# Attention tiles transposed by DMA in six heads, and a new order of VectorE's work, in a graph-attention kernel

## The chip, the cores and the metric

The kernel runs on 1 core of a Trainium2 chip. The metric is the device time of one execution in microseconds; several runs are taken and the median is given. Engines are named as the profile does: PE is TensorE's matmuls, PEld its weight loads, DVE is VectorE, ACT ScalarE, POOL GpSimd, SP SyncE (which here only issues DMAs).

## The reference

A layer of a graph network with masked attention, for 384 nodes, 1024 features and 16 heads of 64. `h` is the normalised input; the mask holds a weight per edge, and minus infinity where there is none.

```python
h = jnp.maximum(_layernorm(x, axis=-1), 0.0)
q = h @ wq.T + bq;  k = h @ wk.T + bk;  v = h @ wv.T + bv
q2 = (q @ wiq.T + biq).reshape(N, H, D).transpose(1, 0, 2)
k2 = (k @ wik.T + bik).reshape(N, H, D).transpose(1, 0, 2)
v2 = (v @ wiv.T + biv).reshape(N, H, D).transpose(1, 0, 2)
scores = jnp.einsum('hnd,hmd->hnm', q2, k2) * scale + mask[None]
attn = jax.nn.softmax(scores, axis=-1)
out = jnp.einsum('hnm,hmd->hnd', attn, v2).transpose(1, 0, 2).reshape(N, OUT_F)
return x + out @ wo.T + bo
```

## The kernel before

Every float32 operand is kept as a high part rounded to float32r and a remainder ("low"), and a product is three matmuls: high by high, high by low, low by high (`mm3`, L373 to L375). A weight chunk (128 x 1024) is loaded by `load` (L68, on SP's queue, into one of four raw buffers), its high part is made by `split_hi` (L80 on ScalarE, or L78 on VectorE) and its remainder by `split_lo` (L85 on VectorE or GpSimd).

The projections q, k, v and v2 come first and end at about 157 us; the mask is built beside them. The prediction and the change are about what follows, the attention loop of `S + LA + 4` steps, S = 48. Step i works on several score tiles at once. A tile is 128 query rows of one head: tile i is part t = i % 3 of head h = i // 3. For tile i the stages are

- `do_S` (L717), in step i: two matmuls into one of two "s" banks of PSUM;
- `do_ttr` (L723, VectorE), in step i + 1: adds the mask, scales, and takes the row minimum of the negated scores; it frees the bank;
- `do_exp` (L727, ScalarE), in step i + 2: exponential and row sum;
- `do_norm` (L740 to L744), in step i + 3: the reciprocal of the sum on VectorE, and then, for a tile that TensorE transposes, the division of the tile on GpSimd (L744);
- for such a tile `do_T` (L764), in step i + 5: three TensorE transposes; and `do_pt`, in step i + 6: the high half as float16 on ScalarE (L771), the remainder on VectorE (L772);
- for a tile that the DMA transposes (`i % 3 in DT`, so t = 0): a scale on VectorE (L742) and `do_high` (L750, ScalarE) in step i + 3, `do_low` (L754, VectorE) in step i + 4, and at the end of that step `do_turn` (L758), which issues one DMA transpose of both halves on SP's queue. The two halves lie in one of three plane slots, `plv[i // 3 % 3]`;
- `do_A` (L779), once per head in step 3h + 9: six matmuls of the transposed tiles with v2; `do_ao` (L789 on ScalarE, L790 on VectorE) one step later; `do_aos` (L794, L795) once per two heads.

Beside the stages of a step, TensorE is given other matmuls by `fill`, a certain amount in each half step: first the q2 and k2 chunks (`fill_qk`, one chunk of 24 matmuls per head), then the output projection (`fill_o`). When a q2 or k2 chunk begins, `qk_head` is put among the tasks, which `run_tasks` runs near the end of the step. It evicts the chunk before (`qk_done`: L383 on ScalarE, L384 on VectorE, and four DMA copies on SP's queue, L579 to L582 or L589), splits the weights of the chunk two further on, and loads the one five further on. From the fourth chunk on, load and `split_hi` come ahead of the eviction.

The output projection adds each of six output tiles in two passes: four chunks of wo into a "g" bank of PSUM, a sum into the residual on VectorE (`ysum`, L669), then four more chunks. There are three "g" banks. `ysums` lists the sums that are due; `flush_y` puts all of them into VectorE's queue, in every step after `do_ttr`, and whenever a bank is about to be used anew. `wo_prep` (steps 37, 40, 42, 44, 47, 51) splits and loads the chunks of wo; the remainders of chunks 2, 3, 4 and 6 are made on GpSimd, that of 5 and 7 on VectorE.

The engines' instruction orders are the order of the Python calls; semaphores between the engines are set by the framework.

Of the kernel before, what the change touches and what calls it, by code (L numbers as in the profile page):

```python
# [25 lines left out]
def gnn_kernel(ctx: ExitStack, tc: tile.TileContext, x, edges, erows, etw, wq, wk, wv, wiq, wik, wiv, wo,  # L26
# [20 lines left out]
    def bank(tag):  # L47
        return psum.tile([128, 512], F32, tag=tag, name=tag, bufs={"g": 3, "a": 1}.get(tag, 2))
# [14 lines left out]
    def load(w):  # L63
        if w >= NCH:
            return
        n, m = chunks[w]
        raw[w] = wpool.tile([128, D], F32, tag="raw", name="raw", bufs=4)
        nc.sync.dma_start(raw[w], W[n][m])  # L68

    def split_hi(w, dst=None, dve=False):  # L70
        if w >= NCH:
            return
        if dst is None:
            t = wpool.tile([128, 2, D], F32R, tag="whl", name="whl", bufs=4)
            dst = (t[:, 0, :], t[:, 1, :])
        whl[w] = dst
        if dve:
            nc.vector.tensor_copy(dst[0], raw[w])  # L78
        else:
            nc.scalar.activation(dst[0], raw[w], AF.Copy)  # L80

    def split_lo(w, eng=None):
        if w < NCH:
            hi, lo = whl[w]
            (eng or nc.vector).tensor_tensor(lo, raw[w], hi.bitcast(F32), OP.subtract)  # L85
# [155 lines left out]
    def mask_select(g):  # L241

        nc.vector.copy_predicated(ma, mbt[g].bitcast(I32), mbt[g])
# [148 lines left out]
    w = 0  # L392
# [201 lines left out]
    def run_tasks():  # L594
        while tasks:
            tasks.pop(0)()

    def qk_head(w):
        first = w - W0 < 3
        if not first:  # L600
            load(w + 5)
            split_hi(w + 2)
        if pendq:
            pendq.pop(0)()
        if 0 < w - W0 < NTAB:
            mask_select(w - W0)
        if first:
            split_hi(w + 2)
        split_lo(w + 2, nc.gpsimd if (w + 2) % 2 == PAR else None)
        if first:  # L610
            load(w + 5)
        if w == W0:
            mask_select(0)

# [17 lines left out]
    W0 = 32  # L632
    WO = NCH - 8

    LT, LA = 5, 7
    DT = (0,)
    PRE, RATE, RATE_O, RATE_E = 84, 7.9, 8, 8
    WSTEPS = (37, 40, 42, 44, 47, 51)
    PAR, OPOOL, ODVE = 1, (2, 3, 4, 6), (2,)
# [16 lines left out]
    def omm(t, h, k, c=(0, 512)):  # L656
        hi, lo = (a[:, h * 512 + c[0]:h * 512 + c[1]] for a in whl[WO + k])
        mm3(oacc[t, h][:, c[0]:c[1]], ao[:, 0, k, t * 128:(t + 1) * 128], ao[:, 1, k, t * 128:(t + 1) * 128],
            hi, lo, k in (0, KH), k in (KH - 1, KT - 1))
# [6 lines left out]
    def ysum(a, c=(0, 512)):  # L666
        t, h = OT[a]
        y = xb[t][:, h * 512 + c[0]:h * 512 + c[1]]
        nc.vector.tensor_tensor(y, oacc[t, h][:, c[0]:c[1]], y, OP.add)  # L669
        return y  # L670

    ysums = []

    def flush_y():
        while ysums:
            ysum(ysums.pop(0))

    def fill_o():


        first = [(0, 0), (0, 1), (1, 0), (1, 1), (2, 0), (2, 1)]
        first += [(a, k) for k in (2, 3) for a in range(3)] + [(a, k) for a in range(3, 6) for k in range(KH)]
        for a, k in first:
            while now[0] < wready[k] or now[0] < 6 * k + OREADY:
                yield 0
            if k == 0:
                flush_y()
                oacc[OT[a]] = bank("g")
            omm(*OT[a], k)
            if k == KH - 1:  # L690
                ysums.append(a)
            yield 4
        bank_step = (0, 0, 0, 49, 50)
        todo = [(a, k) for k in range(KH, 7) for a in range(5)]
        while todo:
            ready = [q for q in todo if now[0] >= max(6 * q[1] + OREADY, wready[q[1]], bank_step[q[0]])]
            if not ready:
                yield 0
                continue
            a, k = ready[0]  # L700
            todo.remove(ready[0])
            if k == KH:
                flush_y()
                oacc[OT[a]] = bank("gggss"[a])
            omm(*OT[a], k)
            yield 4

    st_ps, es, sts, tps, avs, aof = {}, {}, {}, {}, {}, {}
    S = 48

    def do_S(i):
        h, t = divmod(i, 3)
        p, o = divmod(h, 2)
        qs, ks = stacks["q", p], stacks["k", p]
        ps = st_ps[i] = bank("s")
        for s in range(2):
            nc.tensor.matmul(ps[:, :N], qs[:, o, t * 128:(t + 1) * 128], ks[:, o, s, :], start=(s == 0), stop=(s == 1))  # L717

    def do_ttr(i):
        t = i % 3  # L720
        e = es[i] = work.tile([128, N], F32, tag="e", name="e", bufs=EB)
        s = sts[i] = work.tile([128, 4], F32, tag="s", name="s", bufs=12)
        nc.vector.tensor_tensor_reduce(e, st_ps.pop(i)[:, :N], ma[:, t, :], -0.125, 3.0e38, OP.add, OP.min, s[:, 0:1])  # L723

    def do_exp(i):
        s = sts[i]
        nc.scalar.activation(es[i], es[i], AF.Exp, bias=s[:, 0:1], scale=-1.0, accum_out=s[:, 1:2])  # L727

    ptv, plv = [], []
# [8 lines left out]
    def do_norm(i):  # L738
        s = sts[i]
        nc.vector.reciprocal(s[:, 2:3], s[:, 1:2])  # L740
        if i % 3 in DT:
            nc.vector.tensor_scalar(s[:, 2:3], s[:, 2:3], PSC, None, op0=OP.mult)  # L742
        else:
            nc.gpsimd.tensor_tensor(es[i], es[i], s[:, 2:3].to_broadcast([128, N]), OP.mult)  # L744

    planes = {}

    def do_high(i):
        planes[i] = plv[i // 3 % 3]
        nc.scalar.activation(planes[i][:, 0, :], es[i], AF.Copy, scale=sts[i][:, 2:3])  # L750

    def do_low(i):
        pl = planes[i]
        nc.vector.scalar_tensor_tensor(pl[:, 1, :], es.pop(i), sts[i][:, 2:3], pl[:, 0, :], op0=OP.mult, op1=OP.subtract)  # L754
# [6 lines left out]
    def do_T(i):  # L761
        ps = tps[i] = bank("t")
        for k in range(3):
            nc.tensor.transpose(ps[:, k * 128:(k + 1) * 128], es[i][:, k * 128:(k + 1) * 128], ident)  # L764

    def do_pt(i):
        h, t = divmod(i, 3)
        pt = ptv[h % 3]
        hi, lo = (pt[:, s * 3:s * 3 + 3, t * 128:(t + 1) * 128] for s in range(2))
        pv = tps.pop(i)[:, :N].rearrange("p (k n) -> p k n", k=3)  # L770
        nc.scalar.activation(hi, pv, AF.Copy, scale=PSC)  # L771
        nc.vector.scalar_tensor_tensor(lo, pv, PSC, hi, op0=OP.mult, op1=OP.subtract)  # L772

    def do_A(h):
        p, o = divmod(h, 2)
        ps = avs[h] = bank("a")
        for k in range(3):
            for s in range(2):
                nc.tensor.matmul(ps[:, :N], vhl[:, k, h, :, :], ptv[h % 3][:, 3 * s + k, :],  # L779
                                 start=(k == 0 and s == 0), stop=(k == 2 and s == 1))  # L780
# [19 lines left out]
    def fill(n):  # L800
        credit[0] += n
        while credit[0] > 0 and gens:
            try:
                c = next(gens[0])
            except StopIteration:
                gens.pop(0)
                continue
            if c == 0:
                credit[0] = 0.0
                return  # L810
            credit[0] -= c
# [4 lines left out]
    for i in range(S + LA + 4):  # L816
        now[0] = i
        r = RATE if len(gens) == 2 else RATE_O if i < S else RATE_E
        fill(r / 2)
        if i < S:  # L820
            do_S(i)
        fill(r / 2)
        if 0 <= i - 1 < S:
            do_ttr(i - 1)
        flush_y()
        if 0 <= i - 2 < S:
            do_exp(i - 2)
        if 0 <= i - 3 < S:
            do_norm(i - 3)
            if (i - 3) % 3 in DT:  # L830
                do_high(i - 3)
        if 0 <= i - LT < S and (i - LT) % 3 not in DT:
            do_T(i - LT)
        j = i - LA
        if j >= 2 and (j - 2) % 3 == 0 and (j - 2) // 3 < 16:
            do_A((j - 2) // 3)
        if 0 <= i - 4 < S and (i - 4) % 3 in DT:
            do_low(i - 4)
        if 0 <= i - LT - 1 < S and (i - LT - 1) % 3 not in DT:
            do_pt(i - LT - 1)  # L840
        if j >= 3 and (j - 3) % 3 == 0 and (j - 3) // 3 < 16:
            do_ao((j - 3) // 3)
        if j >= 4 and (j - 4) % 6 == 3:
            do_aos((j - 4) // 3)
        run_tasks()
        if 0 <= i - 4 < S and (i - 4) % 3 in DT:
            do_turn(i - 4)
        if i in WSTEPS:
            wo_prep(wp)
            wready[wp] = i + 2  # L850
            wp += 1
    while gens:
        now[0] = 999
        fill(999)


    def finish(a, c=(0, 512)):
# [51 lines left out]
```

## Time and profile before

| what | value |
|---|---|
| times of three runs | 297.25, 297.39, 299.25 us; median 297.39 us |
| the profiled execution | 297.12 us, span 295.4 us, TensorE clock 1.00 |
| PE busy | 287.1 us, 97% of the span |
| DVE, ACT, POOL busy | 214.9, 160.4, 155.6 us |
| HBM read and written | 38.30 and 3.39 MB |

The loop's stretches, busy us of each engine in 20 us:

| stretch | PE | DVE | ACT | POOL | DMA share |
|---|---|---|---|---|---|
| 160 to 180 us | 20.00 | 14.19 | 13.13 | 8.26 | 1.02 |
| 180 to 200 us | 19.58 | 16.30 | 16.21 | 10.66 | 0.75 |
| 200 to 220 us | 19.58 | 16.43 | 15.93 | 7.89 | 0.77 |
| 220 to 240 us | 20.00 | 16.48 | 16.87 | 10.78 | 0.84 |
| 240 to 260 us | 19.74 | 14.81 | 13.82 | 11.85 | 0.70 |
| 260 to 280 us | 18.53 | 16.50 | 13.42 | 10.97 | 0.15 |

The span is the time from the first to the last instruction of the profiled execution; 1.7 us lie around it. Matmuls are pipelined and their ends are modelled, so that a busy PE can still hold short waits; these are seen in the distances between the starts of matmuls. Rows of the timeline give the start, the duration, the engine, the line, the operation with its output and inputs, and in brackets the idle time before it and what ended it. A "q" behind an engine's name is its instruction queue: SPq rows are the issue of a DMA, not its transfer.

### The profile page before, as it was taken

The numbers are of one execution on the slowest core, as the hardware profiler recorded it, in microseconds if no ns is written. First come the engines' busy times: TensorE is split into PE (matmuls) and PEld (weight loads), VectorE is DVE, ScalarE is ACT, GpSimd is POOL, SyncE is SP. The second block draws the span as 40 slices with busy tenths as digits, with TensorE's granted clock in tenths as the row PEclk, the third lists the DMA queues.
The fourth block names the chain that finished last, engine by engine and source line by source line (L and its number), as shares of the span: only waits on it lengthen the run. The fifth ranks groups of instructions, "written<-read, shape, count | busy, mean of one in ns | idle before, by whom it ended". The sixth has DMA issues, their size and how long they took to land.

```text
span 295.4 us, 4837 instructions
## 1 busy us (share of the span) xinstructions
PE 287.1 (97%) x1610; PEld 264.6 (90%) x1610; DVE 214.9 (73%) x509; ACT 160.4 (54%) x291; POOL 155.6 (53%) x153
## 2 busy tenths in 40 slices
PE   6999999999999999999999999999999999989995
PEld 5999999999988889999999999898999998758774
DVE  4958986667754453999875778888888878598723
ACT  3884644234422124335635668787878777459510
POOL 4766666445766888990023445362635357475310
PEclk9999999999999999999999999999999999999999
DMA  7799867982464331386449999777788867811105
GB/s 270 252 327 411 288 192 266 288 279 74 145 214 141 107 118 65 89 275 233 142 126 236 255 249 202 189 175 194 181 201 179 200 159 162 213 29 27 27 2 213
DMA packets 33305, 54.60 MB, mean 185 GB/s; under 512 B 17408, under 2 KB 20992, under 8 KB 33280
## 3 DMA queue, kind: packets, MB, share of 16 engines
q1 hardware_dynamic: 30896, 51.90, 60.8%
q0 software_dynamic: 2064, 1.80, 2.1%
q10 hardware_dynamic: 320, 0.59, 0.8%
q8 instruction: 13, 0.21, 0.3%
q14 instruction: 12, 0.10, 0.1%
HBM read 38.30 MB, written 3.39 MB: 141 GB/s over the span
## 4 chain that ended last, share of the span: by engine, by line
PE 88%; ACT 5%; issue 3%; DVE 2%; DMA 1%; POOL 0%; ACTq 0%
PE g L375 20%; PE g L373 20%; PE g L374 20%; PE s L717 5%; PE a L779 5%; PE t L764 3%; PE s L375 2%; PE s L373 2%; PE s L374 2%; PE g L422 2%; PE t L375 2%; PE t L373 2%; PE t L374 2%; DMA g<-in_x_dram 1%; ACT whl L80 1%
## 5 line engine op out<-in xcount | busy, mean ns | idle before, releaser
L373 PE MATMUL g<-g,whl 128*128 128x384 f32 x312 | 106.8, 342 | 0.0
L375 PE MATMUL g<-g,whl 128*128 128x384 f32 x312 | 104.5, 335 | 0.0
L374 PE MATMUL g<-g,whl 128*128 128x384 f32 x312 | 104.3, 334 | 0.0
L230 POOL DMA_INDIRECT tab<-val,idx x51 | 58.0, 1138 | 33.4 <-issue 11.5
L80 ACT ACTIVATE whl<-raw 128x1024 fp32r<-128x1024 f32 x51 | 53.6, 1053 | 30.0 <-PE g L375 21.1
L85 DVE TENSOR_TENSOR whl<-raw,whl 128x1024 fp32r<-128x1024 f32 x41 | 54.2, 1321 | 17.4 <-ACT whl L80 15.1
L373 PEld LDWEIGHTS g<-g,whl 128*128 128x128 f32 x312 | 58.6, 188 | 0.7
L375 PEld LDWEIGHTS g<-g,whl 128*128 128x128 f32 x312 | 58.6, 188 | 0.3 <-POOL whl L85 0.3
L374 PEld LDWEIGHTS g<-g,whl 128*128 128x128 f32 x312 | 58.6, 188 | 0.0
L744 POOL TENSOR_TENSOR e<-e,s 128x384 f32<-128x384 f32 x32 | 27.6, 864 | 39.0 <-DVE s L740 37.5
L85 POOL TENSOR_TENSOR whl<-raw,whl 128x1024 fp32r<-128x1024 f32 x11 | 26.5, 2411 | 36.8 <-ACT whl L80 33.3
L389 ACT ACTIVATE g<-f,bc 128x384 fp32r<-128x384 f32 x24 | 14.8, 618 | 53.5 <-DVE f L388 39.6
L727 ACT ACTIVATE e<-e,s 128x384 f32<-128x384 f32 x48 | 29.2, 607 | 8.7 <-DVE s L723 7.6
L723 DVE CUSTOM_DVE_ANT_0 e<-s,ma 128x384 f32<-128x384 f32 x48 | 26.4, 551 | 3.0 <-PE s L717 3.0
L717 PE MATMUL s<-ks,qs 128*128 128x384 f32 x96 | 25.1, 342 | 2.3 <-DVE s L723 2.3
L388 DVE TENSOR_TENSOR f<-g,rrow 128x384 f32<-128x384 f32 x24 | 13.3, 553 | 18.0 <-PE g L375 12.0
L717 PEld LDWEIGHTS s<-ks,qs 128*128 128x128 f32 x96 | 17.0, 188 | 5.0 <-DVE s L723 4.2
L384 DVE SCALAR_TENSOR_TENSOR nat<-g,bc,nat 128x384 fp32r<-128x384 f32 x16 | 9.9, 617 | 14.7 <-ACT nat L383 13.6
L754 DVE SCALAR_TENSOR_TENSOR pt<-e,s,pt 128x384 f16<-128x384 f32 x16 | 19.0, 1187 | 1.4 <-ACT pt L750 0.2
L772 DVE SCALAR_TENSOR_TENSOR pt<-t,pt 128x384 f16<-128x384 f32 x32 | 17.4, 544 | 1.9 <-ACT pt L771 1.9
L779 PE MATMUL a<-pt,vhl 128*128 128x384 f16 x96 | 18.2, 326 | 0.0
L390 DVE SCALAR_TENSOR_TENSOR g<-f,bc,g 128x384 fp32r<-128x384 f32 x24 | 16.7, 700 | 0.7 <-ACT g L389 0.7
(166 smaller groups left out, 446.3 us busy)
## 6 DMA issues: line engine op xcount, KB each, us to landing
ks<-nat SPq DMA_DIRECT2D x30, 192.0 KB
raw<-in_wv_dram SPq DMA_DIRECT2D x8, 512.0 KB
raw<-in_wq_dram SPq DMA_DIRECT2D x8, 512.0 KB
raw<-in_wiv_dram SPq DMA_DIRECT2D x8, 512.0 KB
raw<-in_wk_dram SPq DMA_DIRECT2D x8, 512.0 KB
raw<-in_wiq_dram SPq DMA_DIRECT2D x8, 512.0 KB
raw<-in_wik_dram SPq DMA_DIRECT2D x8, 512.0 KB
raw<-in_wo_dram SPq DMA_DIRECT2D x8, 512.0 KB
```

What stands on the lines that cost most here:

```text
L80: nc.scalar.activation(dst[0], raw[w], AF.Copy)
L85: (eng or nc.vector).tensor_tensor(lo, raw[w], hi.bitcast(F32), OP.subtract)
L230: nc.gpsimd.indirect_dma_start(out=tabs[c // RNG], out_offset=bass.IndirectOffsetOnAxis(ap=idx[:, c:c + 1], axis=0), in_=val[:, c:c + 1], ...
L373: nc.tensor.matmul(ps, lhi, rhi, start=first, stop=False)
L374: nc.tensor.matmul(ps, lhi, rlo, start=False, stop=False)
L375: nc.tensor.matmul(ps, llo, rhi, start=False, stop=last)
L717: nc.tensor.matmul(ps[:, :N], qs[:, o, t * 128:(t + 1) * 128], ks[:, o, s, :], start=(s == 0), stop=(s == 1))
L723: nc.vector.tensor_tensor_reduce(e, st_ps.pop(i)[:, :N], ma[:, t, :], -0.125, 3.0e38, OP.add, OP.min, s[:, 0:1])
L727: nc.scalar.activation(es[i], es[i], AF.Exp, bias=s[:, 0:1], scale=-1.0, accum_out=s[:, 1:2])
L744: nc.gpsimd.tensor_tensor(es[i], es[i], s[:, 2:3].to_broadcast([128, N]), OP.mult)
L754: nc.vector.scalar_tensor_tensor(pl[:, 1, :], es.pop(i), sts[i][:, 2:3], pl[:, 0, :], op0=OP.mult, op1=OP.subtract)
L779: nc.tensor.matmul(ps[:, :N], vhl[:, k, h, :, :], ptv[h % 3][:, 3 * s + k, :], start=(k == 0 and s == 0), stop=(k == 2 and s == 1))
```

## The change

Four things change in the attention loop.

- In heads 9 to 14 (tiles 27 to 44) the tile with t = 1 is transposed by DMA as well as the one with t = 0. Its three TensorE transposes, GpSimd's division and the eviction L771 and L772 go, and it has L742, L750, L754 and L758 instead. The plane slots are now given out in turn, tile by tile, instead of head by head.
- `do_low` moves from behind the attention product to just behind `do_ttr`, and so ahead of the step's reciprocal on VectorE.
- `qk_head` has one order for all chunks: eviction, mask selection, `split_hi`, `split_lo`, load.
- `flush_y` no longer runs in every step, and puts only one sum into VectorE's queue when a bank is about to be used anew; what is left is summed after the loop.

```diff
     def qk_head(w):
-        first = w - W0 < 3
-        if not first:
-            load(w + 5)
-            split_hi(w + 2)
         if pendq:
             pendq.pop(0)()
         if 0 < w - W0 < NTAB:
             mask_select(w - W0)
-        if first:
-            split_hi(w + 2)
+        split_hi(w + 2)
         split_lo(w + 2, nc.gpsimd if (w + 2) % 2 == PAR else None)
-        if first:
-            load(w + 5)
+        load(w + 5)
...
-    DT = (0,)
+    def turned(i):
+        return i % 3 == 0 or (27 <= i < 45 and i % 3 == 1)
...
-    def flush_y():
-        while ysums:
+    def flush_y(n=6):
+        for _ in range(min(n, len(ysums))):
             ysum(ysums.pop(0))
...
             if k == 0:
-                flush_y()
+                flush_y(1)
                 oacc[OT[a]] = bank("g")
...
             if k == KH:
-                flush_y()
+                flush_y(1)
                 oacc[OT[a]] = bank("gggss"[a])
...
-    planes = {}
+    planes, pln = {}, [0]
 
     def do_high(i):
-        planes[i] = plv[i // 3 % 3]
+        planes[i] = plv[pln[0] % 3]
+        pln[0] += 1
...
             do_ttr(i - 1)
-        flush_y()
+        if 0 <= i - 4 < S and turned(i - 4):
+            do_low(i - 4)
         if 0 <= i - 2 < S:
             do_exp(i - 2)
...
-        if 0 <= i - 4 < S and (i - 4) % 3 in DT:
-            do_low(i - 4)
...
     while gens:
         now[0] = 999
         fill(999)
+    flush_y()
```

Elsewhere `i % 3 in DT` becomes `turned(i)`.

## The prediction

> **What bounds the kernel now.** I read the page first, then the waits, then the timeline of 158 to 295 us instruction by instruction. Names: tile i is score tile i (48 of them, i = 3h + t, heads h from 0); S(i) its score matmuls (L717), T(i) its three TensorE transposes (L764), ttr(i) the VectorE reduction of it (L723); "step" is one pass of the loop over i. Line numbers are those of before.
>
> ```profile
> PE 287.1 (97%) x1610; PEld 264.6 (90%) x1610; DVE 214.9 (73%) x509; ACT 160.4 (54%) x291; POOL 155.6 (53%) x153
> PE 88%; ACT 5%; issue 3%; DVE 2%; DMA 1%; POOL 0%; ACTq 0%
> ...
> 190.24 0.44 PE L717 MATMUL s<-ks,qs 128*128 128x384 f32 x1 [0.42 <-DVE s L723]
> ...
> 204.65 0.44 PE L717 MATMUL s<-ks,qs 128*128 128x384 f32 x1 [0.42 <-DVE s L723]
> ...
> 262.37 0.44 PE L717 MATMUL s<-ks,qs 128*128 128x384 f32 x1 [1.47 <-DVE s L723]
> ```
>
> TensorE is 97% busy and 88% of the chain, so time comes out by shortening its queue or by removing its few waits. Busy matmuls overlap, so I price TensorE by the distance from one start to the next: 0.174 us for a 384-column matmul, 0.232 for 512 columns, 0.35 for an S pair, 0.33 for a T trio, 0.98 for the six of an attention product A. What exceeds these distances after 158 us is the real stall: 0.58 before 190.24, 0.59 before 204.65, about 0.1 at 218.53, 0.23 at 232.42, 0.43 at 253.29 (on GpSimd's L85) and 1.64 before 262.37: 3.6 us in all. S(i) waits there for ttr(i-2), which frees its PSUM bank. So VectorE, idle a quarter of the span, is nearly co-critical inside the attention loop: it works in lockstep with ScalarE.
>
> ```profile
> 226.16 0.56 DVE L723 CUSTOM_DVE_ANT_0 e<-s,ma 128x384 f32<-128x384 f32 x1
> 226.93 1.25 DVE L754 SCALAR_TENSOR_TENSOR pt<-e,s,pt 128x384 f16<-128x384 f32 x1
> 227.89 0.67 ACT L789 ACTIVATE aot<-a,bc,vsc 64x384 f32<-64x384 f32 x1
> 228.58 1.06 ACT L80 ACTIVATE whl<-raw 128x1024 fp32r<-128x1024 f32 x1
> 229.55 0.56 ACT L383 ACTIVATE nat<-g,bc 128x384 fp32r<-128x384 f32 x1
> 230.14 0.62 DVE L384 SCALAR_TENSOR_TENSOR nat<-g,bc,nat 128x384 fp32r<-128x384 f32 x1 [0.84 <-ACT nat L383]
> 230.68 1.22 DVE L85 TENSOR_TENSOR whl<-raw,whl 128x1024 fp32r<-128x1024 f32 x1
> 231.81 0.55 DVE L723 CUSTOM_DVE_ANT_0 e<-s,ma 128x384 f32<-128x384 f32 x1
> ```
>
> This is step 31: ttr(30) to ttr(31) takes 5.65 us, and S(33) at 232.42 waits for the last row. ScalarE's part starts on its own (its exp at 226.80), independent of ttr(30).
>
> ```profile
> 171.69 0.60 DVE L754 SCALAR_TENSOR_TENSOR pt<-e,s,pt 128x384 f16<-128x384 f32 x1
> 171.85 1.12 POOL L744 TENSOR_TENSOR e<-e,s 128x384 f32<-128x384 f32 x1 [0.94 <-DVE s L740]
> ...
> 257.79 2.39 POOL L85 TENSOR_TENSOR g<-raw,g 128x1024 fp32r<-128x1024 f32 x1 [3.76 <-ACT g L80]
> 258.26 2.34 DVE L754 SCALAR_TENSOR_TENSOR pt<-e,s,pt 128x384 f16<-128x384 f32 x1
> ```
>
> The remainder ("low", L754) has three prices: 0.60 us when it starts ahead of GpSimd's work, 1.25 behind an L744, 2.34 behind an L85 (it ends 0.42 after GpSimd).
>
> ```profile
> 254.06 0.69 DVE L669 TENSOR_TENSOR res<-g,res 128x512 f32<-128x512 f32 x1 [1.12 <-PE g L375]
> 255.11 0.69 DVE L669 TENSOR_TENSOR res<-g,res 128x512 f32<-128x512 f32 x1 [0.36 <-PE g L375]
> ...
> 257.10 0.69 DVE L669 TENSOR_TENSOR res<-g,res 128x512 f32<-128x512 f32 x1 [1.05 <-PE g L375]
> ```
>
> Output sums stand in VectorE's queue before TensorE has finished them: 2.5 us of head-of-line waiting, from which the 1.64 at 262.37 follows.
>
> **Part 1, six T groups less** (tiles 28, 31, 34, 37, 40, 43). TensorE loses 6 x 0.33 = -2.0 us. In exchange ScalarE does a high part (L750, 0.52) for an L771 (0.49), VectorE a low (0.60) and a scale (0.2) for an L772 (0.45), GpSimd loses 6 x 0.83 (L744), SP gains six transposes of about 1.3 us of issue.
>
> **Part 2, q2/k2 eviction ahead of the weight split.** ScalarE's L383 and L80 change places, and VectorE's L384 no longer waits 0.8 to 1.1 us. In heads whose split remainder L85 is on VectorE, that L85 starts when L80 ends: at the 190 us place 187.97 instead of 188.49, so the stall of 0.58 falls to 0.06; the loop between such heads shortens by 0.4 and the 0.59 and 0.1 go too: -1.2 us (nothing at worst, where the q2/k2 chunk ends too late, as at step 31 where its last matmul starts 229.07 to 229.24). In SP's queue the weight load now stands behind the q/k copies and ahead of the turn; it is needed three heads later, some 20 us of other matmuls, so its own lateness is free.
>
> **Part 3, low ahead of the reciprocal.** It saves 0.65 us of low (0.60 for 1.25), which lies off the lockstep until head 9 (VectorE then waits for L383 anyway): 0. In a twice-turned head it hurts: ScalarE's second high part waits for ttr, low, reciprocal and scale in a row. Step 31 again: ttr 226.16, low 226.92 (its high part ends 226.89), scale ends 227.79, high(28) 227.87, L771 228.39, L789 228.88, L383 229.57, L80 230.03 to 231.09, L85 231.12, ttr(31) 232.26 against 231.81. S(33)'s stall grows from 0.23 to 0.68. The same walk through steps 32 to 37 leaves ttr(34) 0.3, ttr(37) 1.0 behind before, and S(39), which TensorE would now reach earlier, stalls 0.32. Together +0.8 us (0 to +1.6).
>
> **Part 4, the plane ring.** Three plane slots now turn over in three tiles instead of three heads: high(31) on ScalarE waits for the transpose of tile 27 to land. SP issued the k copies 230.79 to 233.4; then come the load and the two turns. In before a load issued at 235.00 had moved by about 238.2; one issued at 233.45 ends near 236.6, the transpose, 0.20 MB in 1.0 us, at 237.6, while ScalarE wants the slot at 236.3: up to 1.4 us on the lockstep, with L789, L383 and ttr(34) queued behind. Bounds 0 and +1.4; I take the middle, +0.7, because the landing itself is inferred. The transpose's rate is read from 272 to 280 us (slices of 0.2 us), where the last one ran alone:
>
> ```profile
> GB/s 0 0 0 0 0 0 0 0 0 0 0 0 0 0 8 179 214 218 214 141 10 0 0 0 0 0 0 0 0 0 0 0 0 0 0 0 0 0 0 0
> ```
>
> [...] The row says 179 to 218, and I go by the row.
>
> **Part 5, the tail.** The sums no longer block VectorE, so the 0.43 and 1.64 (-2.1) go; but each sum is now queued only when its bank is wanted, so TensorE waits for all that VectorE has in front of it. Walking from S(39) = 0, with the spacings above and VectorE's own (ttr 0.47, L772 0.45, L790 0.53, L85 1.14, sum 0.64):
> - The cast L78 (step 37) frees GpSimd's L85 just before low(34), which is locked out until 1.9 and ends 2.3; ttr(38) 2.8; S(40) at 3.4 instead of 2.9: +0.53.
> - high(36), low(36), scale, high(37), L789, L790, ttr(40) 7.0: S(42) +0.43. low(37) starts at 7.5, 0.1 ahead of GpSimd's L85 at 7.6: I take the cheap price.
> - ttr(41) 9.0, first sum 9.8, ttr(42) 10.4, low(39) to 11.8, high(40) 12.2, L789, L790, ttr(43) 14.0: S(45) +0.26.
> - Before the second sum VectorE still has low(40), reciprocal, L772 and the L85 of weight 5, whose L80 on ScalarE starts 14.95: L85 16.05, sum 17.2 to 17.85. TensorE wants that bank at 14.9: +2.98. This is the largest term.
> - VectorE then catches up; later low(45) is locked behind another GpSimd L85 and the fifth sum comes 0.8 late: +0.8.
> New waits 5.0; if VectorE came to S(39) without lag, the same walk gives 2.9, and 0 if no sum is late.
>
> **Sum:** -2.0 - 1.2 + 0.8 + 0.7 - 2.1 + 5.0 = +1.2 us on the profiled execution of 297.1 (span 295.4, the rest around it unchanged): 298.3. The median shown, 297.4, is 0.3 above the profiled one: 298.6.
>
> **Rivals.**
> - *The new waits don't form.* For it: VectorE is idle a quarter of the time, low is halved, and GpSimd has room. Against: ScalarE sets the pace of the second sum. Without parts 3 to 5's costs, -2.0 - 1.2 - 0.2 - 2.1 = -5.5: 291.9; with 1 to 2 us of them left 293 to 294.
> - [...] It decides at 0.1 us: if ttr(40) ends later than ScalarE's L80, low(37) ends at 10.4 instead of 8.0, and all VectorE work up to the second sum moves 2.4 us: 301.0, slower. The row at 258.26 is exactly this order. [...]
> - *The turns are later than walked.* SP serves q/k copies, load and two turns in a row; if the full 1.4 us and another 1 us at each of tiles 34 and 37 fall on ScalarE: 298.6 + 0.7 + 2.0 = 301.3. Against: A(9) is at 240.4, 1.6 after its later turn lands.
> - *Gains and waits cancel, or nothing reaches the path:* 297.4.
>
> **How the numbers follow.** A measurement here can tell about 1% (the three times before spread 0.7%): 294.4 to 300.4. My forecast has 0.50 (0.40 inside, 0.09 above, 0.01 below), the first rival 0.20 (0.17 faster, 0.03 inside), GpSimd first 0.14 (0.10 slower, 0.04 inside), late turns 0.06 (0.05 slower, 0.01 inside), cancelling 0.10 (inside): faster 0.18, same 0.58, slower 0.24. The range 293.3 to 301.8 leaves about a tenth out at each end; the forecast's own is 296.5 to 300.4.
>
> **What would show it.** Right: 26 T trios for 32, no S stall near 190 and 204, lows of 0.60 in heads 2 to 8, S(33) still waiting for ttr, and a wait of 2 to 3 us of a 512-column L373 for an L669 near the second sum. Part 4 shows as ScalarE's L750 of tile 31 waiting for a DMA. Wrong: no TensorE wait on L669 at all (then the first rival), or a low of over 2 us at tile 37 (then the second).

## The result and the profile after

The changed kernel is slower: 309.5 us (308.98 to 310.03, four runs), against 297.5 for the kernel before in the same measurement; the ratio is 1.039 (95% interval 1.036 to 1.042). The forecast was 298.6 with a range up to 301.8, so it missed by 11 us. The profiled execution took 309.93 us with a span of 308.2, 12.8 more than the profiled execution before.

In the changed kernel's line numbers the names of the prediction are: S L713, reduction L719, reciprocal L736, scale L738, GpSimd's division L740, high L747, low L751, transpose by DMA L755, T L761, evictions L768 and L769, A L776, aot and aof L786 and L787, sums L665.

The page first; the rows are the busy time and the TensorE clock that was granted, in 40 slices:

```profile
PE 289.6 (94%) x1592; PEld 264.3 (86%) x1592; DVE 215.5 (70%) x515; ACT 160.9 (52%) x291; POOL 151.0 (49%) x147
...
PEclk9999999999999999999999999999999787999999
```

TensorE does 18 instructions less (six T trios) and is yet busy 2.5 us longer: its clock was lower for a while (0.981 in the mean of the span), which the profile before, at 1.00, doesn't show. The waits, as engine, tile and line, what it waited for, and us in total, times, longest:

```profile
ACT pt L747 <- DMA pt<-pt: 6.8, 3, 3.6
...
PE g L373 <- DVE res L665: 3.9, 2, 2.7
PE s L713 <- DVE s L719: 3.8, 3, 2.9
...
PE a L776 <- DVE pt L769: 2.9, 2, 1.5
```

Only the third row has a counterpart before (2.3 us in three waits, the longest 1.5). The timeline round the first loss, heads 9 and 10 (TensorE's own q/k matmuls and some rows left out):

```profile
225.73 0.64 DVE L751 SCALAR_TENSOR_TENSOR pt<-e,s,pt 128x384 f16<-128x384 f32 x1
...
229.73 2.40 SPq L589 DMA_DIRECT2D ks<-nat  x4
...
232.23 0.73 SPq L68 DMA_DIRECT2D raw<-in_wo_dram  x1
...
233.02 2.93 SPq L755 DMA_TRANSPOSE pt<-pt  x2
...
238.34 0.61 ACT L747 ACTIVATE pt<-e,s 128x384 f16<-128x384 f32 x1 [3.56 <-DMA pt<-pt]
238.98 0.67 ACT L786 ACTIVATE aot<-a,bc,vsc 64x384 f32<-64x384 f32 x1
...
239.69 0.61 DVE L787 SCALAR_TENSOR_TENSOR aof<-a,vsc,aot 64x384 f32<-64x384 f32 x1 [4.59 <-ACT aot L786]
240.16 1.05 ACT L80 ACTIVATE whl<-raw 128x1024 fp32r<-128x1024 f32 x1
...
240.83 0.55 DVE L719 CUSTOM_DVE_ANT_0 e<-s,ma 128x384 f32<-128x384 f32 x1
...
241.30 2.81 DVE L751 SCALAR_TENSOR_TENSOR pt<-e,s,pt 128x384 f16<-128x384 f32 x1
241.33 2.36 POOL L85 TENSOR_TENSOR whl<-raw,whl 128x1024 fp32r<-128x1024 f32 x1 [7.10 <-issue]
241.44 0.61 PE L713 MATMUL s<-ks,qs 128*128 128x384 f32 x2 [2.88 <-DVE s L719]
...
244.11 0.53 DVE L769 SCALAR_TENSOR_TENSOR pt<-t,pt 128x384 f16<-128x384 f32 x1
...
244.69 1.76 PE L776 MATMUL a<-pt,vhl 128*128 128x384 f16 x5 [1.44 <-DVE pt L769]
```

Read it from the top. The low of tile 27 is done at 226.4, but its transpose stands on SP's queue behind the four k copies, which are issued only from 229.73, and a weight load. It is the first of the two issued from 233.02 (the ninth transpose in the trace, at 226.26, is tile 24's, held up in the same way). ScalarE's high part of tile 31 wants that plane slot and stands idle from 234.78 for 3.56 us (its scale is done at 235.1, so that some 3.2 of these are the slot's alone). Behind it in ScalarE's order stand the aot, the q2 eviction and the weight split; VectorE waits 4.59 us for the aot, and so its next reduction comes at 240.83 and S(36) starts 2.88 us late (3.05 by the starts of matmuls). Then a second loss follows at once: the low of tile 31 meets GpSimd's L85, which starts 0.03 us after it, is locked out and takes 2.81 us (it ends 0.42 after L85; alone, the lows of this trace take 0.61 or 0.62), and the attention product waits 1.44 us for the eviction behind it.

By the starts of matmuls, as in the prediction, TensorE's waits after 158 us, counting those over 0.3, come to 13.6 us (3.2 before), of which 3.05, 1.82, 0.89 and 1.67 lie between 241 and 257 us, 1.46 is a wait for GpSimd's L85, and 2.92 and 1.41 are waits for sums. Matmuls at wide distances, in two stretches after 242 us, add 3.7 us. The windows show what these are; the columns are the stretch, its length, the busy time of PE, PEld, DVE, ACT and POOL with the instructions, the granted clock, the DMA share and GB/s:

```profile
242.00:242.04 0.04, 0.04 (x2) 0.04 (x1) 0.04 (x1) 0.04 (x1) 0.04 (x1) 1.00 0.01 0
242.04:248.87 6.83, 5.39 (x19) 4.03 (x18) 4.68 (x12) 1.95 (x6) 2.48 (x2) 0.50 0.82 172
248.87:249.00 0.13, 0.13 (x2) 0.13 (x1) 0.00 (x0) 0.00 (x0) 0.00 (x0) 1.00 0.08 10
...
255.69:259.10 3.41, 2.93 (x9) 1.95 (x9) 2.50 (x10) 1.69 (x4) 1.78 (x2) 0.50 1.04 208
```

The clock is granted at half from 242.04 to 248.87 and again from 255.69 to 259.10. From the first score matmul to the last matmul the changed kernel takes 143.8 us and the kernel before 131.6: 10.4 of waits and 3.7 of slow matmuls more, 2.0 of T trios less, 12.1. The rest of the 12.8 lies ahead of the loop (0.3) and behind the last matmul (0.4).

### The profile page after: what moved, and what is told of

It is laid out like the page before. It is cut to its first block, busy times and chain, and to the rows that moved or that the text cites. A ratio compares the mean times of both kernels' runs of the same rounds, so it can differ in the third digit from the quotient of the medians.

```text
span 308.2 us, 4816 instructions
## 1 busy us (share of the span) xinstructions
PE 289.6 (94%) x1592; PEld 264.3 (86%) x1592; DVE 215.5 (70%) x515; ACT 160.9 (52%) x291; POOL 151.0 (49%) x147
## 5 line engine op out<-in xcount | busy, mean ns | idle before, releaser
L230 POOL DMA_INDIRECT tab<-val,idx x51 | 59.0, 1157 | 33.0 <-issue 11.1
L80 ACT ACTIVATE whl<-raw 128x1024 fp32r<-128x1024 f32 x51 | 53.6, 1051 | 29.5 <-PE g L375 21.1
L85 DVE TENSOR_TENSOR whl<-raw,whl 128x1024 fp32r<-128x1024 f32 x41 | 54.3, 1324 | 18.5 <-ACT whl L80 17.7
L85 POOL TENSOR_TENSOR whl<-raw,whl 128x1024 fp32r<-128x1024 f32 x11 | 26.6, 2416 | 48.6 <-ACT whl L80 30.4
L740 POOL TENSOR_TENSOR e<-e,s 128x384 f32<-128x384 f32 x26 | 21.5, 828 | 47.3 <-DVE s L736 33.8
L713 PE MATMUL s<-ks,qs 128*128 128x384 f32 x96 | 25.4, 346 | 3.8 <-DVE s L719 3.8
L719 DVE CUSTOM_DVE_ANT_0 e<-s,ma 128x384 f32<-128x384 f32 x48 | 26.4, 551 | 3.6 <-PE s L713 2.9
L747 ACT ACTIVATE pt<-e,s 128x384 f16<-128x384 f32 x22 | 13.6, 616 | 27.1 <-issue 11.8
L787 DVE SCALAR_TENSOR_TENSOR aof<-a,vsc,aot 64x384 f32<-64x384 f32 x16 | 9.9, 616 | 19.3 <-ACT aot L786 18.9
L776 PE MATMUL a<-pt,vhl 128*128 128x384 f16 x96 | 20.4, 349 | 2.9 <-DVE pt L769 2.9
L713 PEld LDWEIGHTS s<-ks,qs 128*128 128x128 f32 x96 | 17.5, 193 | 6.4 <-DVE s L719 5.5
L751 DVE SCALAR_TENSOR_TENSOR pt<-e,s,pt 128x384 f16<-128x384 f32 x22 | 20.7, 939 | 1.8 <-ACT pt L747 1.4
L769 DVE SCALAR_TENSOR_TENSOR pt<-t,pt 128x384 f16<-128x384 f32 x26 | 14.3, 550 | 9.1 <-ACT pt L768 9.1
```

What stands on the lines that cost most here:

```text
L230: nc.gpsimd.indirect_dma_start(out=tabs[c // RNG], out_offset=bass.IndirectOffsetOnAxis(ap=idx[:, c:c + 1], axis=0), in_=val[:, c:c + 1], ...
```

## The experiments

The theory after this reading: what costs is the second turned tile, by two mechanisms that the prediction had too small or at another place, the plane slots (theory 1) and GpSimd's lock on the low. The rival is that the other three edits, the sums above all, make the loss.

**A fourth plane slot.**

```diff
+        plv.append(work.tile([128, 2, N], F16, tag="pl4", name="pl4", bufs=1))
-        planes[i] = plv[pln[0] % 3]
+        planes[i] = plv[pln[0] % 4]
-            aof[p] = work.tile([128, N], F32, tag="aof", name="aof")
+            aof[p] = work.tile([128, N], F32, tag="aof", name="aof", bufs=1)
```

> The changed kernel with a fourth plane slot (the buffer of the attention output, aof, goes from two copies to one to make room), so that the high part of tile 31 reuses the slot of tile 24 instead of tile 27. Theory 1, the plane ring: ScalarE's high parts no longer wait for a DMA transpose (6.8 us in three waits before), TensorE does not stand idle 2.9 us at 241 us, its clock is not granted at half for the 7 us after it, and the time falls from 309.5 to about 302 (300 to 304): 3.05 and 0.89 of stalls and about 3.5 of slow clock less. Theory 2, output sums and the order of VectorE set the loss: no more than 1 us less, 308 to 310. Theory 3, the transposes themselves land too late for the attention products: the wait moves to L776, and the time stays above 305.

Measured: 305.4 us, ratio 1.026 (1.021 to 1.031). No high part waits for a DMA, S(36) isn't late, and the half clock at 242 is gone: the mechanism of theory 1 is there. But the gain of 4 us is a third of the loss, less than expected. The timeline of this kernel (its lines are one further on) shows the rest:

```profile
238.18 2.83 DVE L752 SCALAR_TENSOR_TENSOR pt<-e,s,pt 128x384 f16<-128x384 f32 x1
238.22 2.38 POOL L85 TENSOR_TENSOR whl<-raw,whl 128x1024 fp32r<-128x1024 f32 x1 [3.95 <-issue]
...
241.59 0.97 PE L777 MATMUL a<-pt,vhl 128*128 128x384 f16 x5 [1.63 <-DVE pt L770]
```

The low of tile 31 starts 0.04 us ahead of GpSimd's L85 and still lasts 2.83. The second turned tile's low stands right behind the weight split of the step before, so it meets L85 where that is GpSimd's: 2.83, 2.53 and 2.77 us in heads 10 to 12, and TensorE's products wait 1.63 and 1.48 behind the first two.

**No second turned tile; the other edits stay.**

```diff
-        return i % 3 == 0 or (27 <= i < 45 and i % 3 == 1)
+        return i % 3 == 0
```

> The changed kernel with turned(i) cut to i % 3 == 0: no tile of t = 1 is transposed by DMA; the new eviction order, the low ahead of the reciprocal and the sums on demand stay. Theory 1: without the second turned tile a plane slot is reused three heads later, no high part waits, the clock stays whole: 297.5 - 1.2 (eviction order) + about 3 (sums on demand, 4.3 of waits for 2.1 before) = 299, between 297 and 301. Theory 2: nearly all of the loss stays, 305 to 309.

Measured: 296.3 us, ratio 0.9945 (0.992 to 0.997), clock 1.00. The three other edits together are a gain; the expectation's 3 us for the sums were wrong.

**The old way of the sums in the changed kernel.**

```diff
             do_ttr(i - 1)
+        flush_y()
```

with `flush_y` taking all sums, as before.

> The changed kernel with the output sums put into VectorE's queue as before, in every step. Theory 1: the plane waits and the slow clock stay; TensorE's waits for L665 (2.9 and 1.4 us) go and before's head-of-line waits of about 2 come back: 306.5 to 309. Theory 2: the sums are most of the loss, 299 to 302.

Measured: 310.8 us, ratio 1.042 (1.037 to 1.047): no gain, and theory 2 falls. The two waits for sums are gone, and as much waiting came elsewhere (13.6 us in all, as in the changed kernel).

**The second turned tile alone, in the kernel before.** The edit is `turned` and the new way of giving out slots.

> The kernel before with only the second turned tile in heads 9 to 14 and the plane slots given out tile by tile; old eviction order, old place of the low, old sums. Theory 1: the slot waits come with this part alone: 302 to 307, with a high part that waits 2 to 4 us for a DMA transpose and a granted clock below 1 behind it. Theory 2 (the reordering makes the loss, the turned tiles are a gain): six T groups less, 295 to 297.5.

Measured: 308.8 us, ratio 1.039 (1.033 to 1.045), nearly all of the loss. It overshot the expectation in time, and the slot waits fell short of the 2 to 4 us expected: high parts wait 4.2 us for transposes in three waits, the longest 1.9. Two lows last 2.46 and 2.47, and TensorE's score matmuls wait 5.6 us for VectorE, 2.3 in the kernel before. So the loss comes with the second turned tile, but its parts are other ones under the old order.

**The transposes ahead of the copies and the load on SP's queue.**

```diff
+        if 0 <= i - 4 < S and turned(i - 4):
+            do_turn(i - 4)
         run_tasks()
-        if 0 <= i - 4 < S and turned(i - 4):
-            do_turn(i - 4)
```

> The changed kernel, three plane slots as it has, with do_turn ahead of run_tasks, so that on SP's queue the transposes stand ahead of the q/k copies and the weight load. If their place in that queue makes the slot wait, ScalarE's high parts wait under 1 us for a DMA transpose, and the time falls to that with a fourth slot, about 305 (303 to 307), since the second cost, the low of t = 1 locked behind GpSimd's L85 (2.8, 2.5 and 2.8 us with four slots, with TensorE's products waiting 1.6, 1.5 and 2.3 behind it), is untouched. If the transfers themselves are slow whatever stands ahead of them, the waits of 2 to 4 us stay, and 307 to 310.

Measured: 304.2 us, ratio 1.022 (1.018 to 1.026), with three slots and no wait of a high part for a DMA. The SP rows:

```profile
226.21 1.22 SPq L755 DMA_TRANSPOSE pt<-pt  x1
229.55 2.39 SPq L589 DMA_DIRECT2D ks<-nat  x4
```

The row at 226.21 is tile 27's now, the tenth transpose, 6.8 us earlier than in the changed kernel. So the slot wait came from the place in the queue, behind the copies and the load; issued ahead of them, the transfers are fast enough. The lows of 2.83 and 2.53 us are untouched, as expected.

**The low of the second turned tile ahead of the weight split** (with four slots):

```diff
-        if 0 <= i - 4 < S and turned(i - 4):
+        if 0 <= i - 4 < S and (i - 4) % 3 == 0:
             do_low(i - 4)
...
+        if 0 <= i - 3 < S and (i - 3) % 3 == 1 and turned(i - 3):
+            do_low(i - 3)
         if j >= 3 and (j - 3) % 3 == 0 and (j - 3) // 3 < 16:
             do_ao((j - 3) // 3)
```

> The changed kernel with the fourth plane slot, and the low of the second turned tile (t = 1) one step earlier: behind its own high part and ahead of that step's weight split, not one step after it. If the lock of that low behind GpSimd's L85 is the second cost: its lows cost 0.6 us, the waits of 1.6, 1.5 and 2.3 us of TensorE and the slow clock behind the last go, and the time is 296 to 299. If the remaining 9 us with four slots come from the number of instructions on ScalarE and VectorE or from the transfers, it stays at 303 to 306.

Measured: 301.0 us, ratio 1.010 (1.006 to 1.014). All six moved lows take 0.61 or 0.62 us, and no product waits for an eviction behind one; 4.4 us go, short of the expected 6 to 9. Left are a wait of 1.6 us for L85 in step 40, one of 3.1 for a sum (1.5 with four slots alone) with 3.4 us of half clock beside it, and a product's wait of 0.7 for its DMA transpose.

**Early low and early transpose, three slots:** `do_low(i - 3)` as above, and `do_turn` for both tiles ahead of `run_tasks`.

> The changed kernel with three plane slots, the low of the second turned tile one step earlier, its transpose in that step too, and all transposes ahead of the step's q/k copies and load on SP's queue. [...] If the slots still turn over too fast: 299 to 303. If the extra transposes cost by their traffic: over 300.

Measured: 300.3 us (299.86 to 302.76), ratio 1.008 (1.005 to 1.011). Had the slot wait and the low's long time beside L85 been the whole loss, six T groups less (2 us of TensorE) beside the 296.3 without the second turned tile would have given 294 to 297. The time is that expected for slots that turn over too fast, though no slot is waited for. The profiled execution took 302.65, which is 2.3 above the median, so that its waits are those of a slower run than the median one. Step 40 in it:

```profile
248.69 1.25 DVE L751 SCALAR_TENSOR_TENSOR pt<-e,s,pt 128x384 f16<-128x384 f32 x1 [0.26 <-ACT pt L747]
...
250.29 0.62 ACT L747 ACTIVATE pt<-e,s 128x384 f16<-128x384 f32 x1 [1.03 <-issue]
...
251.62 1.06 ACT L80 ACTIVATE whl<-raw 128x1024 fp32r<-128x1024 f32 x1
...
252.81 2.35 POOL L85 TENSOR_TENSOR whl<-raw,whl 128x1024 fp32r<-128x1024 f32 x1 [2.00 <-issue]
...
255.22 0.50 PE L374 MATMUL g<-whl,g 128*128 128x512 f32 x1 [1.99 <-POOL whl L85]
```

The low of the first turned tile lasts 1.25 us beside a division on GpSimd; reciprocal and scale of the second wait behind it, so its high part, the weight split and GpSimd's remainder are late, and TensorE needs that remainder.

**Sums as before, without the second turned tile:** the edit of the third experiment on the second.

> The changed kernel without the second turned tile and with the sums put into VectorE's queue in every step as before, so that only the new eviction order and the low ahead of the reciprocal are left. In the run without the second turned tile TensorE waits 1.08 and 0.43 us for a sum on demand; the kernel before has 1.47 at the same place from sums that block VectorE. So sums on demand are worth nothing here: 296.3, within 0.7. If they are worth what the prediction's fifth part took off (2.1) without its cost: 298. If on-demand sums cost 1.5: 295.

Measured: 296.4 us, ratio 0.993 (0.990 to 0.996), the same as with sums on demand.

**The first turned tile's low behind reciprocal, scale and high part,** on top of early low and early transpose:

```diff
-        if 0 <= i - 4 < S and (i - 4) % 3 == 0:
-            do_low(i - 4)
...
             if turned(i - 3):
                 do_high(i - 3)
+        if 0 <= i - 4 < S and (i - 4) % 3 == 0:
+            do_low(i - 4)
```

> The kernel with early low and early turn of the second turned tile, and besides the low of the first turned tile behind the step's reciprocal, scale and high part instead of ahead of them. What is left there is a wait of 2.0 us of TensorE for GpSimd's L85 in step 40 and waits for sums. If the row of VectorE work ahead of the second high part (reduction, low, reciprocal, scale) is what makes ScalarE's L80 and with it GpSimd's L85 late (L80 starts 2.6 us after the attention product, 0.7 without the second turned tile), that wait falls below 1.2 and the time from 300.3 to about 299 (298 to 299.7). If not: 300 to 301.

Measured: 295.3 us, ratio 0.993 (0.991 to 0.996): the gain is more than twice what was expected.

```profile
247.01 0.67 ACT L786 ACTIVATE aot<-a,bc,vsc 64x384 f32<-64x384 f32 x1
247.71 1.06 ACT L80 ACTIVATE whl<-raw 128x1024 fp32r<-128x1024 f32 x1
...
251.35 0.50 PE L374 MATMUL g<-whl,g 128*128 128x512 f32 x1 [0.33 <-POOL whl L85]
```

L80 in step 40 starts 0.7 us after the attention product's last matmul, no longer 2.6, and the wait for L85 falls from 1.99 to 0.33. The lows themselves got dearer in places (1.20 to 1.26 us in three early heads, 2.25 at 253.48), without any wait of TensorE from it. The waits are 2.9 us in all and the clock is whole, while in the profiled run of the kernel it came from it was halved twice for 3.4 us, at 256 and 266 us. The runs of that kernel near its median have a mean clock of 0.994, which is one such stretch, and 3.4 us at a granted clock of 0.50 lose at most 1.7, by estimate; so of the 5 us between the two medians no more than 1.7 are slow clock. The rest is waits that are gone and what the two measurements differ by; these weren't separated.

**The same kernel as in the last run, with sums as before.**

> The kernel before it in this list with the sums put into VectorE's queue in every step. The waits for sums (1.8 and 0.4 us, and the slow clock behind the first) go, and one or two waits of a score matmul for VectorE of 1.5 us come: within 1.5 us of that kernel. If the sums on demand are what keeps it above 296: 296 to 297.

Measured: 296.7 us, ratio 0.997 (0.995 to 1.000), 1.4 us above the kernel of the last run and so within the 1.5 expected; one score matmul waits 1.87 us for VectorE, and the clock is halved once, at 263. With the second turned tile in this order sums on demand are, if anything, a small gain.

**The eviction order alone, and the low's place alone, in the kernel before.**

> The kernel before with only the new order in qk_head (eviction, mask, split, load). As predicted for this part alone: the score matmuls at 190 and 204 us no longer wait 0.58 and 0.59 us, and the time is 1.2 us less, a ratio of 0.996. Rival: the low ahead of the reciprocal made the gain of 1 us, and this part gives nothing, a ratio of 0.999 to 1.001.

> The kernel before with only the low moved ahead of the reciprocal. As predicted, where one tile per head is turned its saving lies beside other work: a ratio of 0.999 to 1.001, with lows of 0.6 us for 1.25 in heads 2 to 8. Rival: it makes the gain, 0.996.

Measured: 296.2 us, ratio 0.997 (0.995 to 0.999), for the eviction order, its stalls at 190 and 204 gone; 297.4 us, ratio 1.0005 (0.998 to 1.003), for the low, those stalls at 0.58 each as before. Both came out as predicted.

The steps from the changed kernel (each ratio is to the runs of before that stood beside it), each with the waits of TensorE after 158 us and the stretches of half clock of its profiled execution:

| kernel | us | ratio to before | waits, us | half clock, us |
|---|---|---|---|---|
| changed | 309.5 | 1.039 | 13.6 | 6.8 and 3.4 |
| transposes ahead of copies and load | 304.2 | 1.022 | 10.1 | 3.4 |
| and low of t = 1 early | 300.3 | 1.008 | 5.1 | 3.4 and 3.4 |
| and low of t = 0 behind the high part | 295.3 | 0.993 | 2.9 | none |
| changed, without the second turned tile | 296.3 | 0.9945 | 2.3 | none |

Beside the second and third rows the kernel before had a median of 298.7 us, beside the others 297.4 or 297.5, so the steps into and out of these rows hold to about 1 us: by the ratios they are 5.1, 4.0 and 4.5 us. The fixes were tried in this one order; what each would give first is not known. The version in the fourth row beats both kernels, the one before by 0.7% (0.4 to 0.9); from the fifth it can't be told apart by these runs.

## Why the prediction was wrong, step by step

Every sign that was to show the forecast right is there: 26 T trios, no stall near 190 and 204, short lows in heads 2 to 8, S(33) waiting, a long wait for the second sum, tile 31's high part waiting for a DMA. The time is still 11 us off. The signs tested where the waits would be, and not how long they are or what each sets off.

- **Part 1, six T groups: right, and small.** 18 TensorE instructions are gone, and the last version's PE is busy 284.4 us, 286.3 without the second turned tile.
- **Part 2, the eviction order: right.** -1.2 was forecast; the run of this part alone gives a ratio of 0.997, 0.8 us less (0.3 to 1.4).
- **Part 3, low ahead of the reciprocal: half right.** With one turned tile it is worth nothing, as forecast. With two, +0.8 (at most +1.6) was far too small. The stall of S(33), 0.37 us for 0.68, was even smaller than walked. The mechanism was named (the second high part waits for reduction, low, reciprocal and scale), but the walk followed only the reduction and S. It did not follow ScalarE's order on to L80, GpSimd's L85 and the wo matmul that needs it. Putting the low back gave 5.0 us (4.5 by the ratios), at most 1.7 of it slow clock, in a kernel with the early low and the early transpose; alone it wasn't tried.
- **Part 4, the plane ring: the step that failed first.** The place and the mechanism were right; the size was not. The wait is 3.56 us, the bound was 1.4. Counted from the issue of the first k copy (230.79 in the walk, 229.73 in the run), ScalarE wants the slot after 5.05 us where 5.5 was walked, and has it after 8.6 where 6.8 was. The 1.8 us are mis-sized transfers: the walk had the weight load moved 3.15 us after its issue and then one transpose alone in 1.0. By the DMA packets of the trace the load, issued at 232.23, begins at 234.08, while the last packets of the k copies move (to 234.63), and ends at 237.02, 4.8 us after its issue, and the packets of both transposes move side by side from 235.90 to 238.39. (In before, too, the last packet of the load issued at 235.00 ended at 239.28, not at 238.2.) What mattered more is what stood behind it: the wait was added to the sum as itself, while S(36) stalls 3.05 us, the clock is then halved, and the same happens again, smaller, at the next heads. Undoing it by the order on SP's queue gives 5.3 us (5.1 by the ratios). The third rival, late turns at a chance of 0.06, named this: it priced 1.4 us and twice 1 more, and the three waits are 3.56, 2.77 and 0.48.
- **The lock on the low: right as a price, wrong as a place and in its margin.** The second rival, GpSimd's L85 ahead of low(37), asked for it at tile 37, and it didn't happen there: that low starts 0.18 us ahead of GpSimd's L85 and takes 0.61. Part 5 had it at tile 34, where it is 2.53 us. The other large ones, 2.27 at tile 39 and 2.81 at tile 31, weren't walked. The one at tile 31 is behind the split of a wo chunk that `qk_head` runs. I had asked where the low meets L85 for S alone; the eviction L769 stands behind it too, and A waits for that. The margin of 0.1 us was also read too boldly: in before itself nine lows started 0.01 to 0.03 us ahead of an L744 and took 1.25 to 1.27 each. In the traces of before, of the changed kernel and of the one with four slots, the lows that started 0.16 to 0.18 us ahead of a GpSimd instruction took 0.60 or 0.61, and those 0.01 to 0.04 ahead took 1.25 to 2.83 and ended 0.41 or 0.42 after GpSimd's; no low in the first two led by 0.04 to 0.15. So who started first in the trace didn't decide at the small leads. The run with the earlier low shows what it is worth to start well ahead, 0.62 for 2.83 us.
- **Part 5, the sums: the row was right, the balance wrong.** The second sum's wait was forecast at 2.98 and is 2.92; the later one 0.8 and is 1.41. But the comparison with sums as before gives 296.3 and 296.4 us without the second turned tile, so on demand costs as much as it saves there, and the +2.9 net of this part was no property of the sums: VectorE's lateness showed up at whichever instruction TensorE asked for next.
- **Not in the sum at all: the clock.** 3.7 us in the changed kernel.

## What to carry to other kernels

When a ring of buffers is made to turn over faster, look up when the transfer that frees a slot is *issued*, behind which waiting copies on its queue, and which transfers move beside it, before estimating how long it takes. Follow a delayed instruction through everything behind it on its own engine, to each engine that waits for one of those, and not only to the next score matmul. Put an operation that another engine can lock out, as L85 did the low (2.83 us for 0.62), well ahead of the point that releases the other one. And ask of a sign not only whether it is there, but how large it would be if the forecast held.

## What the runs showed of the hardware

While TensorE had work, its granted clock fell to half in stretches of 3.41 us, or 6.83, and never for another length, after stalls that were short: 2.88 us (from 242.04), 2.27 with a fourth slot (from 258.06), 1.49 with the transposes ahead (from 250.44). Yet a stall of 2.66 us before 274.24 in the changed kernel was followed by none.

The traces' clock records show more. Within a trace the falls start whole multiples of 3.41 us apart: 4 in the changed kernel, 7 and 3 with sums as before, 3 with early low and early transpose. Cut at these times, TensorE's time after 158 us can be sorted by the share of each piece that it stood idle (distances of matmul starts less the usual spacings). In the eight traces that have a fall all twelve pieces ahead of one were idle for 57 to 88%, and no other piece at full clock for more than 57%. The stall before 274.24 is split by such a time, 272.76, into pieces idle for 42 and 48%. At 57% the two meet: the piece from 263.01 to 266.42 with early low and early transpose is followed by a fall, the one from 264.09 to 267.50 with the transposes ahead is not. So neither the length of one stall nor a limit of the idle share tells the cases apart in these traces, and no run was made to test one.

In such a stretch matmuls of 512 columns start 0.43 us apart, outside it 0.23 (early low and early transpose, at 266.76 and at 263.29 us). A stretch of 3.41 us at a granted clock of 0.50 loses, by estimate, at most half its length, 1.7 us, on top of the stall; the 10.2 us of them in the changed kernel lost 3.7.
